# Layer norm's two averages: products of 128 contraction rows, or of 64 on the two halves of the array

## The chip, the cores and the metric

The kernel runs on one core of a Trainium2 chip. A core has TensorE (PE; its weight loads are shown as PEld), VectorE (DVE), ScalarE (ACT), GpSimd (POOL) and SyncE (SP), which run their own instruction streams in order and wait for one another by semaphores. The metric is device time in microseconds, the median of several runs.

## The reference

Input x is 32 images of 128 channels, 32 x 32 points, in fp32. There are two layers, each added to its input:

```python
def _layernorm(x, gamma, beta, eps=1e-05):
    mu = jnp.mean(x, axis=-1, keepdims=True)
    var = jnp.var(x, axis=-1, keepdims=True)
    return (x - mu) * jax.lax.rsqrt(var + eps) * gamma + beta
...
# layer 0, on the group norm of x: u is (32, 128, 1024)
h = jnp.einsum('bdl,de->ble', u, W_enc) + b_enc        # 1024 features
y = gelu(causal convolution of h over the points, 64 taps per feature, + D * h)
g = y @ W_glu + b_glu
g = g[..., :D_MODEL] * jax.nn.sigmoid(g[..., D_MODEL:])
h = _layernorm(h + g, ln_gamma, ln_beta)
out = h @ W_dec + b_dec                                # back to 128 channels
...
# layer 1, on the group norm of the result: a deformable convolution with 64 taps,
# its offsets from a 3 x 3 depthwise convolution, then batch norm and gelu
```

The change concerns `_layernorm` in layer 0: for each of an image's 1024 points, the mean and the mean square over 1024 features.

## The kernel before, in words

A first stage (`ssm_convolution`, up to about 1500 us) makes the convolved features y and puts them into DRAM. Then `main_block` runs two generators side by side: `first_part(b + 2)`, the rest of layer 0 for one image, and `second_part(b)`, the deformable convolution of the image two before it.

`first_part` takes an image in two halves of 512 points (`hf`). A half has eight groups m of 128 features. For each m, TensorE makes the gate (`gpg`, L757, eight matmuls), a decode matmul of the group before (`gpo`, L685), the value (`gpv`, L780, eight matmuls) and the encoding h again (`gph`, L796). ScalarE takes the sigmoid of the gate (L764). VectorE makes gate times value in L788 (`gs`, from `gpv`) and adds h in L809. The result r, 128 features x 512 points, is summed over m on GpSimd: `sums[0]` adds r (L687, in `decode`), and `sums[1]` adds r squared (L818, from ScalarE's square of L817). After eight groups `sums[0]` and `sums[1]` hold, on 128 partitions, partial sums that must still be added over the partitions. `close` does that with two matmuls whose weights `davg` are all 1/1024, so that each of 128 output rows holds the mean: `gpm` (L707) for the mean and `gpq` (L710) for the mean square. ScalarE copies the mean to SBUF (L708) and squares it (L711). The rest of the norm follows in later steps: L714, L717, a root, reciprocals, L726, L729.

A half's `close` is not run at its end but in the next half's group m = 0, after the value's matmuls and L788, and before `gph`. Tile names there: `pglu` has three PSUM banks that gate, value, the two averages and h take in turn. After a close, `gph` and the gate of m = 1 (`gpg`) therefore take the banks that L788 and L708 have read. Temporaries (`temp`) come from five buffers.

`second_part` goes through 68 pieces per image. A piece's weights `ds` (hat functions that ScalarE wrote to DRAM in L953 to L955 and SyncE loads back in L1029) are multiplied by `dhy` on VectorE (L1048). Three matmuls (`dps`, L1091, 208 to 480 columns) go into the four banks of `psam`, VectorE multiplies each by tap weights on the way out (L1094), and GpSimd adds halves (L1111) and then into the image's accumulator (L1116). At the end of an image GpSimd scales the accumulator (L1122) and VectorE adds the input (L1127).

The order of all instructions is that of the program text, under `manual_schedule`. How the two generators interleave is decided by `run_along`: each yields a cost, and the one that has done the smaller share of its total goes on. `MM` is the cost of one 512-column matmul, and

```python
FIRST = 2 * (KD * (2 * KD + 2) + 2) * MM
```

is the total of `first_part`. `tick` runs the steps that `later` has put off by a number of yields.

Of the kernel before, what the change touches and what calls it, by code (L numbers as in the profile page):

```python
# [7 lines left out]
F32 = mybir.dt.float32  # L8
# [6 lines left out]
P = 128  # L15
# [3 lines left out]
KD = D // P  # L19
# [526 lines left out]
def main_block(nc, tc, const, ins, x, u_d, y_d, x1_d, out, offmax):  # L546
# [16 lines left out]
    T = 512  # L563
# [4 lines left out]
    with ctx:  # L568

        def pool(name, bufs, space=None):  # L570
            kw = {} if space is None else {"space": space}
            return ctx.enter_context(tc.tile_pool(name=name, bufs=bufs, **kw))
# [8 lines left out]
        pglu = pool("mb_pg", 3, PSUM)  # L581
# [42 lines left out]
        for k in range(KD):  # L624
            nc.tensor.matmul(
                fold[:, 0:1], w_dec[:, k, :], beta[:, k : k + 1],
                start=(k == 0), stop=(k == KD - 1),
# [32 lines left out]
        MM = 863.0  # L660
# [3 lines left out]
        def load(n, chunks):  # L664

            if n >= len(tiles):
                return
            b, hf = tiles[n]
            cols = slice(hf * T, hf * T + T)
            if n not in loaded:  # L670
                u = two.tile([P, T], F32, tag="gu", name=f"gu_{b}_{hf}")
                nc.sync.dma_start(u, u_d[b, :, cols])
                loaded[n] = u, []
            src = y_d[:, b].rearrange("d j l -> d (j l)")[:, cols]
            for k in chunks:
                y = ypool.tile([P, T], F32, tag="gy", name=f"gy_{b}_{hf}_{k}")
                nc.sync.dma_start(y, src[k * P : (k + 1) * P])
                loaded[n][1].append(y)

        def temp(name):  # L680
            return tpool.tile([P, T], F32, tag="gt", name=name)

        def decode(job):
            m, r, sums, dec = job
            nc.tensor.matmul(dec, w_dec[:, m, :], r, start=(m == 0), stop=(m == KD - 1))  # L685
            if m > 0:
                nc.gpsimd.tensor_add(sums[0], sums[0], r)  # L687
# [7 lines left out]
        def tick():  # L695
            for e in list(soon):
                e[0] -= 1
                if e[0] <= 0:
                    soon.remove(e)
                    e[1]()  # L700

        def close(b, hf, sums, dec, xt):

            tag = f"{b}_{hf}"
            m1, d, rs = (temp(f"g{n}_{tag}") for n in ("m1", "d", "rs"))
            ps = pglu.tile([P, T], F32, tag="g", name=f"gpm_{tag}")
            nc.tensor.matmul(ps, const["davg"], sums[0], start=True, stop=True)  # L707
            nc.scalar.copy(m1, ps)  # L708
            ps = pglu.tile([P, T], F32, tag="g", name=f"gpq_{tag}")
            nc.tensor.matmul(ps, const["davg"], sums[1], start=True, stop=True)  # L710
            nc.scalar.activation(rs, m1, AF.Square)  # L711

            def variance():
                nc.vector.scalar_tensor_tensor(  # L714
                    d, m1, neg_g, dec, op0=ALU.mult, op1=ALU.add
                )
                nc.vector.tensor_sub(rs, ps, rs)  # L717

            def deviation():
                nc.scalar.activation(rs, rs, AF.Sqrt, bias=const["eps"])  # L720

            def invert(lo):
                return lambda: nc.vector.reciprocal(rs[:, lo : lo + P], rs[:, lo : lo + P])

            def scale():
                nc.vector.tensor_mul(d, d, rs)  # L726

            def add():
                nc.vector.scalar_tensor_tensor(xt, d, shift, xt, op0=ALU.add, op1=ALU.add)  # L729

            def store():
                nc.scalar.dma_start(x1_d[b, :, hf * T : hf * T + T], xt)
                stored.add((b, hf))

            later(2, variance)
            later(4, deviation)
            for n in range(4):
                later(7 + n, invert(n * P))
            later(11, scale)
            later(12, add)  # L740
            later(15, store)

        stored = set()
        pending = {}

        def first_part(b, last=False):
            for hf in range(2):
                n = tiles.index((b, hf))
                if n == 0:
                    load(0, range(KD))  # L750
                u, ys = loaded.pop(n)
                sums = dec = xt = None
                for m in range(KD):
                    tag = f"{b}_{hf}_{m}"
                    gate = pglu.tile([P, T], F32, tag="g", name=f"gpg_{tag}")
                    for k in range(KD):
                        nc.tensor.matmul(  # L757
                            gate, w_glu[:, k, D + m * P : D + m * P + P], ys[k],
                            start=(k == 0), stop=(k == KD - 1),
                        )  # L760
                        yield MM
                        tick()
                    sig = temp(f"gs_{tag}")
                    nc.scalar.activation(  # L764
                        sig, gate, AF.Sigmoid, bias=b_glu[:, KD + m : KD + m + 1]
                    )
                    if m == 1:
                        load(n + 1, range(YB - KD))
                        dec = pdec.tile([P, T], F32, tag="dec", name=f"gpo_{b}_{hf}")
                        pending["decode"] = (0, r0, sums, dec)  # L770
                    if m == 4:
                        xt = one.tile([P, T], F32, tag="gx", name=f"gx_{b}_{hf}")
                        nc.sync.dma_start(xt, x[b, :, hf * T : hf * T + T])
                    if "decode" in pending:
                        decode(pending.pop("decode"))
                        yield MM
                        tick()
                    val = pglu.tile([P, T], F32, tag="g", name=f"gpv_{tag}")
                    for k in range(KD):
                        nc.tensor.matmul(  # L780
                            val, w_glu[:, k, m * P : m * P + P], ys[k],
                            start=(k == 0), stop=(k == KD - 1),
                        )
                        if m == KD - 1 and k < 2 * KD - YB:
                            load(n + 1, [YB - KD + k])
                        yield MM
                        tick()
                    nc.vector.scalar_tensor_tensor(  # L788
                        sig, val, b_glu[:, m : m + 1], sig, op0=ALU.add, op1=ALU.mult
                    )  # L790
                    if "close" in pending:
                        close(*pending.pop("close"))
                        yield 2 * MM
                        tick()
                    h = pglu.tile([P, T], F32, tag="g", name=f"gph_{tag}")
                    nc.tensor.matmul(  # L796
                        h, w_enc[:, m * P : (m + 1) * P], u, start=True, stop=True
                    )
                    yield MM
                    tick()  # L800
                    if m == 0:
                        sums = [
                            one.tile([P, T], F32, tag=f"gs{i}", name=f"gs{i}_{b}_{hf}")
                            for i in range(2)
                        ]
                        r = sums[0]
                    else:
                        r = two.tile([P, T], F32, tag="gr", name=f"gr_{tag}")
                    nc.vector.scalar_tensor_tensor(  # L809
                        r, h, b_enc[:, m : m + 1], sig, op0=ALU.add, op1=ALU.add  # L810
                    )
                    if m == 0:
                        nc.scalar.activation(sums[1], r, AF.Square)
                        r0 = r
                    else:
                        sq = temp(f"gq_{tag}")
                        nc.scalar.activation(sq, r, AF.Square)  # L817
                        nc.gpsimd.tensor_add(sums[1], sums[1], sq)  # L818
                        pending["decode"] = (m, r, sums, dec)
                pending["close"] = (b, hf, sums, dec, xt)  # L820
            if last:
                decode(pending.pop("decode"))
                close(*pending.pop("close"))
                while soon:
                    yield MM
                    tick()

        FIRST = 2 * (KD * (2 * KD + 2) + 2) * MM


        images = {}
# [322 lines left out]

        ctx.enter_context(tc.manual_schedule())
        run_along((first_part(0), FIRST))
        run_along((first_part(1), FIRST), (opening(), 90.0))
        for b in range(B):
            steps = prepare(b + 1) if b + 1 < B else []
            if b + 2 < B:  # L1160
                run_along(
                    (first_part(b + 2, last=(b + 2 == B - 1)), FIRST),
                    (second_part(b, steps), SECOND),
# [154 lines left out]
```

## Time and profile before

| | |
|---|---|
| time, median of 3 runs (lowest to highest) | 13582.52 us (13579.27 to 13584.45) |
| the profiled execution: span from first to last instruction | 13587.2 us |
| the profiled execution's own time beside the span | not listed apart; the span is 4.7 us above the median |
| TensorE busy | 13106.8 us, 96% of the span |
| VectorE busy | 8781.8 us, 65% |
| ScalarE busy | 3291.8 us, 24% |
| GpSimd busy | 9080.3 us, 67% |
| mean granted TensorE clock | 0.988 of full speed |
| mean busy share of the DMA engines, 2500 to 13000 us | 0.87 |

How to read the views. In a timeline a row has the start (us from the span's start), the length, the engine, the line, the operation, out<-in, the shape of the tile and a count of merged instructions; in brackets stands the engine's idle time ahead of the row and what ended it. An fp32 matmul appears as two instructions (x2), one for each pass, and a pass's end is modelled, so the pitch from one row's start to the next is a better length for TensorE than the row's own. In the view of waits a row has who waited for whom, the total in us, how many times, and the longest one. In a view of one line the three numbers are the shortest, the median and the longest instruction in ns.

### The profile page before, as it was taken

The page shows a single profiled execution, that of the slowest core. Times are in us where ns is not written, and L with a number is a line of the kernel's source. Part 1 is how long each engine was busy: PE and PEld are TensorE (multiplying, and loading weights), DVE is VectorE, ACT ScalarE, POOL GpSimd, SP SyncE. Part 2 cuts the span into 40 slices and gives each one's busy share as a digit, 9 for nine tenths or more (in the row PEclk, how much of TensorE's full clock was granted, in tenths as well). Part 3 has the DMA queues.
Part 4 walks back from the last instruction along what each step waited for, and adds up shares of the span by engine and source line. Part 5 has one row for each costly group of instructions (what it writes and reads, how often), then busy time and mean ns, then how long its engine had stood idle before and what let it go on. Part 6 is the DMA issues. An engine that isn't in the chain of part 4 may idle for free.

```text
span 13587.2 us, 133930 instructions
## 1 busy us (share of the span) xinstructions
PE 13106.8 (96%) x40482; PEld 7248.5 (53%) x40482; DVE 8781.8 (65%) x12685; ACT 3291.8 (24%) x4767; POOL 9080.3 (67%) x8868
## 2 busy tenths in 40 slices
PE   7999899999999999999999999999999999999975
PEld 7888545555555555555555555555555555555533
DVE  7787226666666666666666666666666666666677
ACT  4333222222211122222222211112222222221145
POOL 2444227777777777777777777777777777777778
PEclk9999999999999999999999999999999999999988
DMA  7888428888888888888889888888888888988876
GB/s 244 275 277 273 132 90 231 234 239 236 231 227 231 233 235 238 238 236 232 230 234 239 235 229 229 231 232 237 238 237 236 232 230 235 240 235 231 230 198 175
DMA packets 1715626, 3105.77 MB, mean 229 GB/s; under 512 B 308306, under 2 KB 1018322, under 8 KB 1713874
## 3 DMA queue, kind: packets, MB, share of 16 engines
q1 hardware_dynamic: 1502290, 2641.91, 73.2%
q10 hardware_dynamic: 163456, 320.92, 6.6%
q0 software_dynamic: 49152, 134.28, 2.9%
q8 instruction: 329, 5.39, 0.2%
q14 instruction: 399, 3.27, 0.1%
HBM read 2630.36 MB, written 466.06 MB: 228 GB/s over the span
## 4 chain that ended last, share of the span: by engine, by line
PE 81%; DMA 9%; DVE 4%; ACT 2%; POOL 2%; issue 1%; SPq 1%; ACTq 0%; DVEq 0%; POOLq 0%
PE gpv L780 24%; PE gpg L757 23%; PE dps L1091 23%; DMA ds<-dhat 4%; PE gph L796 3%; PE gpo L685 3%; PE psy L299 3%; PE psz L223 2%; DMA y_d<-yo 2%; DMA dhat<-dh 2%; DVE z L227 1%; DVE ds L1048 1%; DMA dhy<-dhat 1%; POOL y_d L332 1%; ACT ds L1040 0%
## 5 line engine op out<-in xcount | busy, mean ns | idle before, releaser
L1094 DVE TENSOR_TENSOR dp<-dps,k_weight_slots 128x256 f32<-128x256 f32 (+17 forms) x6528 | 3087.1, 483 | 3109.5 <-PE dps L1091 2914.8
L1091 PE MATMUL dps<-ds,dxw 128*128 128x256 f32 (+18 forms) x13056 | 4701.1, 447 | 223.5 <-DVE ds L1048 177.5
L1116 POOL TENSOR_TENSOR dacc<-dacc,dp 128x256 f32<-128x256 f32 (+3 forms) x4736 | 4417.4, 933 | 396.5 <-DVE dp L1111 26.6
L1091 PEld LDWEIGHTS dps<-ds,dxw 128*128 128x128 f32 x13056 | 2472.7, 192 | 3203.6 <-issue 2537.5
L757 PE MATMUL gpg<-gy,g_w_glu 128*128 128x512 f32 x8192 | 3986.4, 593 | 23.5 <-DMA gy<-y_d 15.7
L780 PE MATMUL gpv<-gy,g_w_glu 128*128 128x512 f32 x8192 | 3975.7, 592 | 0.0
L1111 POOL TENSOR_TENSOR dp<-dp 128x448 f32<-128x448 f32 (+2 forms) x2142 | 2675.1, 1249 | 1882.1 <-DVE dp L1094 1879.4
L1048 DVE TENSOR_TENSOR ds<-ds,dhy 128x1024 f32<-128x1024 f32 (+3 forms) x2176 | 3148.6, 1447 | 762.4 <-DMA ds<-dhat 647.9
L757 PEld LDWEIGHTS gpg<-gy,g_w_glu 128*128 128x128 f32 x8192 | 1546.9, 190 | 1235.8 <-issue 964.9
L780 PEld LDWEIGHTS gpv<-gy,g_w_glu 128*128 128x128 f32 x8192 | 1551.7, 190 | 1155.3 <-issue 913.8
L818 POOL TENSOR_TENSOR gs<-gs,gq 128x512 f32<-128x512 f32 x448 | 628.5, 1403 | 1341.3 <-ACT gq L817 1341.3
L817 ACT ACTIVATE gq<-gr 128x512 f32<-128x512 f32 x448 | 282.3, 630 | 4673.6 <-DVE gr L809 4611.2
L332 POOL DMA_DIRECT2D y_d<-yo x1024 | 590.1, 583 | 869.7 <-ACT yo L320 699.2
L764 ACT ACTIVATE gs<-gpg,k_b_glu 128x512 f32<-128x512 f32 x512 | 351.8, 687 | 2488.0 <-PE gpg L757 2377.6
L953 ACT ACTIVATE dh<-dr,k_minus 128x624 f32<-128x624 f32 x768 | 621.7, 809 | 642.5 <-DMA dhat<-dh 563.1
L299 PE MATMUL psy<-toe,z 128*128 128x192 f32 x4096 | 704.7, 333 | 45.2 <-ACT yo L320 43.8
L299 PEld LDWEIGHTS psy<-toe,z 128*128 128x128 f32 x4096 | 667.5, 192 | 81.6 <-ACT yo L320 74.5
L311 DVE TENSOR_TENSOR psy<-psy,t 32x256 f32<-32x256 f32 (+1 forms) x1280 | 553.7, 433 | 204.7 <-ACT t L307 162.6
L788 DVE SCALAR_TENSOR_TENSOR gs<-gpv,k_b_glu,gs 128x512 f32<-128x512 f32 x512 | 379.7, 742 | 437.3 <-PE gpv L780 437.2
L687 POOL TENSOR_TENSOR gs<-gs,gr 128x512 f32<-128x512 f32 x448 | 634.7, 1417 | 0.0
L954 ACT ACTIVATE dh<-dh,one 128x624 f32<-128x624 f32 x768 | 626.3, 815 | 25.0
L223 PE MATMUL psz<-w_enc,u 128*128 128x128 f32 x4096 | 568.6, 293 | 44.9 <-DVE z L227 32.3
(162 smaller groups left out, 6052.4 us busy)
## 6 DMA issues: line engine op xcount, KB each, us to landing
dhy<-dhat SPq DMA_DIRECT2D x1536, 512.0 KB
ds<-dhat SPq DMA_DIRECT2D x1440, 512.0 KB
dhat<-dh ACTq DMA_DIRECT2D x768, 312.0 KB
y_d<-yo POOLq DMA_DIRECT2D x1024, 128.0 KB, 5.4
gy<-y_d SPq DMA_DIRECT2D x512, 256.0 KB
u<-u_d SPq DMA_DIRECT2D x224, 512.0 KB
toe<-kp_d SPq DMA_DIRECT2D x128, 768.0 KB
dxw<-dvt_d SPq DMA_DIRECT2D x1248, 64.0 KB
```

The lines of the kernel that those rows point to most:

```text
L223: nc.tensor.matmul(ps[:, j, :], u[:, lo : lo + P], w_enc[:, k * P : (k + 1) * P], start=True, stop=True,)
L299: nc.tensor.matmul(ps[:, c // 2, c % 2, :], rows[i][:, g * CG + c0 + c, :], toe[:, c0 + c, :], start=True, stop=True,)
L332: nc.gpsimd.dma_start(y_d[d0 : d0 + CG, :, i * NB + ORDER[j], :].rearrange("d b l -> b d l"), yo[i][j * B : (j + 1) * B],)
L687: nc.gpsimd.tensor_add(sums[0], sums[0], r)
L757: nc.tensor.matmul(gate, w_glu[:, k, D + m * P : D + m * P + P], ys[k], start=(k == 0), stop=(k == KD - 1),)
L780: nc.tensor.matmul(val, w_glu[:, k, m * P : m * P + P], ys[k], start=(k == 0), stop=(k == KD - 1),)
L818: nc.gpsimd.tensor_add(sums[1], sums[1], sq)
L1048: nc.vector.tensor_mul(s[:, :m], s[:, :m], hy[:, :m])
L1091: nc.tensor.matmul(ps, xw[:, j, :], s[:, :m, :, y0 : y0 + ny], start=True, stop=True)
L1094: nc.vector.tensor_mul(prod[:, :m, :, y0 : y0 + ny], ps, w[:, :, :, None].to_broadcast([P, m, KY2, ny]),)
L1111: adder.tensor_add(prod[:, :m, 0], prod[:, :m, 0], prod[:, :m, 1])
L1116: nc.gpsimd.tensor_add(to, to, prod[:, slot : slot + nj, 0])
```

## The change

Before the averages, a new step `halve` folds the running sums onto half of the partitions: ScalarE copies the upper 64 partitions of `sums[0]` to the lower 64 of a temporary, and the lower 64 of `sums[1]` to its upper 64. VectorE adds the temporary onto the lower half of `sums[0]` and onto the upper half of `sums[1]`. The mean is then a matmul over partitions 0 to 63 and the mean square one over partitions 64 to 127. `halve` is called in group m = 0 of the next half, after the fifth of the value's eight matmuls. Both products are recorded ahead of the copy of the mean, `close` yields one `MM` in place of two, and the total `FIRST` goes down with it.

```diff
+        HP = P // 2
+
+        def halve(b, hf, sums, dec, xt):
+
+            other = temp(f"gf_{b}_{hf}")
+            nc.scalar.copy(other[:HP], sums[0][HP:])
+            nc.scalar.copy(other[HP:], sums[1][:HP])
+            nc.vector.tensor_add(sums[0][:HP], sums[0][:HP], other[:HP])
+            nc.vector.tensor_add(sums[1][HP:], sums[1][HP:], other[HP:])
+
         def close(b, hf, sums, dec, xt):
...
-            ps = pglu.tile([P, T], F32, tag="g", name=f"gpm_{tag}")
-            nc.tensor.matmul(ps, const["davg"], sums[0], start=True, stop=True)
-            nc.scalar.copy(m1, ps)
+            pm = pglu.tile([P, T], F32, tag="g", name=f"gpm_{tag}")
             ps = pglu.tile([P, T], F32, tag="g", name=f"gpq_{tag}")
-            nc.tensor.matmul(ps, const["davg"], sums[1], start=True, stop=True)
+            nc.tensor.matmul(pm, const["davg"][:HP], sums[0][:HP], start=True, stop=True)
+            nc.tensor.matmul(ps, const["davg"][HP:], sums[1][HP:], start=True, stop=True)
+            nc.scalar.copy(m1, pm)
             nc.scalar.activation(rs, m1, AF.Square)
...
+                        if m == 0 and k == 4 and "close" in pending:
+                            halve(*pending["close"])
                         yield MM
                         tick()
...
                         close(*pending.pop("close"))
-                        yield 2 * MM
+                        yield MM
                         tick()
...
                 decode(pending.pop("decode"))
+                halve(*pending["close"])
                 close(*pending.pop("close"))
...
-        FIRST = 2 * (KD * (2 * KD + 2) + 2) * MM
+        FIRST = 2 * (KD * (2 * KD + 2) + 1) * MM
```

## The prediction

> **What bounds the kernel now.** I read the page first: span, busy shares, the chain that ended last.
>
> ```profile
> span 13587.2 us, 133930 instructions
> ...
> PE 81%; DMA 9%; DVE 4%; ACT 2%; POOL 2%; issue 1%; SPq 1%; ACTq 0%; DVEq 0%; POOLq 0%
> ```
>
> TensorE holds the end, so any pass taken off it looks like time won. But the two products sit in a place of their own: one "close" per half image, 64 in all. So I asked next what TensorE waits for near them, in the view of waits (total us, times, longest).
>
> ```profile
> PE gph L796 <- DVE gs L788: 30.6, 29, 2.4
> ...
> PE gpg L757 <- DVE gs L788: 7.5, 10, 0.9
> ```
>
> L796 is the matmul right behind the two products, L757 the one behind that. Both wait for VectorE's L788 (gate times value). To see which close waits how, I read the timeline at every close. Apart from the first three and the last there are two kinds, 30 of each.
>
> Kind A closes the first half of an image. TensorE and VectorE at 6246 us:
>
> ```profile
> 6246.27 1.02 PE L707 MATMUL gpm<-gs,davg 128*128 128x512 f32 x2
> 6247.12 1.02 PE L710 MATMUL gpq<-gs,davg 128*128 128x512 f32 x2
> 6247.98 0.66 PE L1091 MATMUL dps<-ds,dxw 128*128 128x288 f32 x2
> 6249.95 1.13 PE L796 MATMUL gph<-gu,k_W_enc 128*128 128x512 f32 x2 [1.31 <-DVE gs L788]
> ```
>
> ```profile
> 6247.18 1.23 DVE L1048 TENSOR_TENSOR ds<-ds,dhy 128x1024 f32<-128x1024 f32 x1 [1.66 <-DMA ds<-dhat]
> 6248.32 0.91 DVE L1094 TENSOR_TENSOR dp<-dps,k_weight_slots 128x256 f32<-128x256 f32 x2
> 6249.16 0.74 DVE L788 SCALAR_TENSOR_TENSOR gs<-gpv,k_b_glu,gs 128x512 f32<-128x512 f32 x1
> ```
>
> The products take 0.85 us each. TensorE is through with them and the 288-column matmul, stands still 1.31 us, and goes on 0.05 us after L788 ends (6249.90). L788 in turn hangs on a DMA that VectorE awaited at L1048.
>
> Kind B closes the second half. VectorE, GpSimd and TensorE at 6431 us:
>
> ```profile
> 6426.95 1.13 DVE L1048 TENSOR_TENSOR ds<-ds,dhy 128x832 f32<-128x832 f32 x1 [0.34 <-DMA ds<-dhat]
> 6428.00 0.38 DVE L1094 TENSOR_TENSOR dp<-dps,k_weight_slots 128x224 f32<-128x224 f32 x1
> 6428.30 1.85 DVE L1127 TENSOR_TENSOR do<-do,dxr 128x1024 f32<-128x1024 f32 x1
> 6430.07 0.58 DVE L1094 TENSOR_TENSOR dp<-dps,k_weight_slots 128x420 f32<-128x420 f32 x1
> 6431.95 0.56 DVE L1094 TENSOR_TENSOR dp<-dps,k_weight_slots 128x390 f32<-128x390 f32 x1 [1.30 <-POOL dacc L1116]
> 6432.44 1.46 DVE L1048 TENSOR_TENSOR ds<-ds,dhy 128x832 f32<-128x832 f32 x1
> 6433.82 0.74 DVE L788 SCALAR_TENSOR_TENSOR gs<-gpv,k_b_glu,gs 128x512 f32<-128x512 f32 x1
> ```
>
> ```profile
> 6427.16 1.91 POOL L1111 TENSOR_TENSOR dp<-dp 128x448 f32<-128x448 f32 x1
> 6429.15 2.78 POOL L1116 TENSOR_TENSOR dacc<-dacc,dp 128x64 f32<-128x64 f32 x4
> ```
>
> ```profile
> 6433.64 1.02 PE L796 MATMUL gph<-gu,k_W_enc 128*128 128x512 f32 x2
> 6434.61 1.13 PE L757 MATMUL gpg<-gy,g_w_glu 128*128 128x512 f32 x2
> ```
>
> L796 would free TensorE at 6434.50; L757 starts at 6434.61, 0.05 us after L788 ends (6434.56). So L788 is late here too, by 0.11 us in this close and by up to 0.94 us in others. The chain behind it is GpSimd (4.72 us for L1111 and L1116), then the evict of 390 columns, L1048, L788. Both kinds go on when L788 ends, not when the products end.
>
> **What the change removes.** Two products of 0.85 us, four passes of 0.43 us one after another (1.71 us). No row shows two products at once. Bounds: all side by side, 0.86 us; as now, 1.71 us. I need not choose, because neither end reaches the clock: in A and B TensorE waits for L788 either way. In A the wait only grows. In B it opens in front of L757. Value on the path: 0. In the first three closes (no second stream beside them) another cover holds: L796 writes the bank that L708 frees, L708 ends 1.65 us after gpm starts, L796 starts at 1.72. At most 0.05 us each is to be had.
>
> The Trainium skill, "TensorEngine Tiling (Array Packing)", Key Properties, says that tiles on different row groups run independently, but that changing the tiling mode drains the array, which speaks against a change that switches twice per close. By the first, the removed part would be worth up to 0.43 to 0.85 us per close if it were on the path; by the second, something goes back. No row here shows either.
>
> **What it moves.** The built programs differ in order: one yield less puts the second stream (dps) one slot later against the first. In A the order becomes gpm, gpq, gph, dps. The 288-column matmul, 0.48 us at the pitch of 0.85 us per 512 columns, now does its work in the wait; after the change it comes behind it: +0.48 us per A. Cover: some 14 us later TensorE stands again for an evict (L1094) that is late through a DMA, 0.5 us or more in 15 of the 29 A closes that I read, 1.02 us in this one. Where it stands, the 0.48 is swallowed. Half of them: 0.24 x 30 = 7 us. SyncE's order changes in 60 or so pairs of loads by one place against gy, gu and gx loads; all are issued ahead, so 0.
>
> **What it adds.** Per close, two ScalarE copies and two VectorE adds, all on 64 partitions x 512.
>
> Copies: nearest row L1040, a copy on 32 partitions, 0.62 us at its shortest. ScalarE sat idle 8 to 9 us before L708 in B; in A the copies stand behind a hat's two activations that end 4 to 8 us before gpm, and ahead of the one that waits for its DMA. They wait for GpSimd's last L687, which ends about 8 us ahead of gpm in A, 3 to 4 in B. VectorE reaches the adds 2 to 3 us ahead of gpm in B, so it waits 0 to 0.3 us for the first copy. Cost 0.
>
> Adds: nearest row L726, two SBUF inputs, 128x512: 691 ns shortest, 1049 longest. Alone two cost 1.4 us, beside a busy GpSimd 2.1.
>
> In A they stand before the idle that ended with the DMA: 1.66 us here, 1.1 to 3.2 elsewhere. They lie in it with at most 0.1 us over on average: 30 x 0.1 = 3 us.
>
> In B they go between L1048 (ends 6428.08) and the evict of 224 columns, with the 1.30 us idle as cover. That is gone (2.0 against 1.30), and the cover is itself GpSimd's lateness, which grows: L1111 of 448 took 1.13 us at 6422.85 beside evicts alone, and 1.91 beside L1048 and L1127. L1111 with its four L1116 took 3.08 us there and 4.72 here, with 2.7 us of VectorE's two-input work beside it: 0.6 us lost for each. Two adds more, 2 us, make GpSimd about 1.1 us later, so the 390-column evict, L1048, L788 and L757 too. Low end: GpSimd loses nothing, 2.0 - 1.30 with adds at 0.7 leaves 0.1 us. High end: adds 2.1 on top of a late sum, 1.5 us. I take 1.0, nearest to the row that shows both engines busy: 30 x 1.0 = 30 us. TensorE has no stall behind it in B that would give it back.
>
> Queued behind the adds on VectorE are the evicts that free the four psam banks; the order leaves three matmuls of slack, so no stall there. The last close (tail) gets the folding in series, about 2 us once, off the chain.
>
> **Sum.** 30 + 7 + 3 = 40 us. On the profiled execution, 13587.2 + 40 = 13627. That span is 4.7 us above the median of the three runs (13582.5), and nothing outside the span changes: 13622 us.
>
> **Rivals.** (1) Hidden: GpSimd does not mind and the idles cover the adds. B 0.1, A 0 to 0.24: 3 to 10 us more, 13586 to 13593. For it: 1.30 us of idle against 1.4 of work. Against: GpSimd's rows of 1.13 and 1.91.
> (2) Faster: the saved pass reaches the end. 64 x 0.43 = 27 us, with both 64 x 0.85 = 55: 13528 to 13555. It decides if L788 ends before the shortened products do, which in none of the 60 closes it does now. It would take a shift of the interleave that clears A's wait.
> (3) Worse: in B the first copy waits on GpSimd's late sum, VectorE stands, and A's 0.48 is nowhere swallowed: B 1.5, A 1.0: 75 us, 13657.
> (4) The change does not do what it says: both products run one after another as now. Then the time is that of my forecast all the same, since the saving is hidden; only the rows would tell.
>
> **How the numbers follow.** About 0.2%, 27 us, is what a measurement of this kernel can tell from no change. Forecast (20 to 60 us) 0.58, hidden 0.27, faster 0.07, worse 0.08. Of the forecast about a tenth lies below 27 us: slower 0.60, same 0.33, faster 0.07. The range reaches from the hidden case's low end to just past the worse case's: 13582 to 13660.
>
> **What would show it.** Right: L788 still the releaser in front of L796 in A, and now of L757 in B, with that second total well above 7.5 us; gpg after gph later in B by about 1 us; adds of 0.7 to 1.05 us; the second product starting 0.43 us or less after the first, or at 0.85, with the same time. GpSimd's L1111 and L1116 in B longer than 4.72 us together. Wrong: L757 and L796 starting without an idle ahead, or the stall in B unchanged at about 0.1 us.

## The result, and the profile after

The changed kernel takes 13624.7 us (median of six runs, 13610.73 to 13640.13) against 13582.52 us before (13579.27 to 13586.29): 42 us slower, ratio 1.0032 with a 95% interval of 1.0021 to 1.0044. That is 0.3%, small but clear of the interval. The forecast was 13622. That it came out within 3 us is partly luck: its terms for the closes of kind A were wrong, and what they left out largely cancelled; the experiments take this apart.

The profiled execution of after is the slowest of its six, so its span is 51 us above that of before. Its span and busy times:

```profile
span 13638.4 us, 134143 instructions
...
PE 13118.4 (96%) x40482; PEld 7231.1 (53%) x40482; DVE 8953.8 (66%) x12813; ACT 3367.4 (25%) x4895; POOL 9179.3 (67%) x8868
```

VectorE does 172 us more work than before (adds, and slower neighbours) and GpSimd 99 us more with the same instructions. TensorE's products became shorter and its busy time still went up by 12 us.

In after, line numbers have moved: the copies are L707 and L708, the adds L709 and L710, the products L718 and L719, and old L757, L788, L796, L1048, L1094, L1111 and L1116 are now L767, L800, L808, L1061, L1107, L1124 and L1129. The view of waits of after (who waits for whom: total us, times, longest):

```profile
PE gph L808 <- DVE gs L800: 62.7, 30, 2.9
PE gpg L767 <- DVE gs L800: 32.1, 28, 1.8
...
PE dps L1104 <- DVE dp L1107: 4.4, 8, 1.5
```

The first row was 30.6 us, the second 7.5. Gate times value (L800) is still the releaser in A, and now also in front of `gpg` 28 times, with the close shown next as the pattern, as the prediction asked. The third row, TensorE's second stall some 14 us behind an A close, was 31.1 us (51 times) before.

A close of kind B in the timeline of after (start, length, engine, line; in brackets the idle time ahead and what ended it):

```profile
6440.64 1.91 POOL L1124 TENSOR_TENSOR dp<-dp 128x448 f32<-128x448 f32 x1
...
6441.49 1.61 DVE L709 TENSOR_TENSOR gs<-gs,gf 64x512 f32<-64x512 f32 x1
...
6442.63 3.66 POOL L1129 TENSOR_TENSOR dacc<-dacc,dp 128x64 f32<-128x64 f32 x4
6443.13 0.70 DVE L710 TENSOR_TENSOR gs<-gs,gf 64x512 f32<-64x512 f32 x1
...
6444.72 0.69 PE L718 MATMUL gpm<-gs,davg 64*128 64x512 f32 x1
6444.73 0.69 PE L719 MATMUL gpq<-gs,davg 64*128 64x512 f32 x1
6445.25 0.59 PE L718 MATMUL gpm<-gs,davg 64*128 64x512 f32 x1
6445.26 0.59 PE L719 MATMUL gpq<-gs,davg 64*128 64x512 f32 x1
...
6446.33 0.56 DVE L1107 TENSOR_TENSOR dp<-dps,k_weight_slots 128x390 f32<-128x390 f32 x1 [0.44 <-POOL dacc L1129]
...
6448.19 0.74 DVE L800 SCALAR_TENSOR_TENSOR gs<-gpv,k_b_glu,gs 128x512 f32<-128x512 f32 x1
...
6448.98 1.12 PE L767 MATMUL gpg<-gy,g_w_glu 128*128 128x512 f32 x2 [0.88 <-DVE gs L800]
```

The two products lie on each other: the second starts 0.01 us after the first, and the next pair of passes 0.53 us later, so all four passes take 1.06 us in place of 1.71. Nothing comes of it. On VectorE one of the adds takes 1.61 us; GpSimd's L1124 and L1129, beside them, take 5.65 us from first start to last end, where L1111 and L1116 took 4.77; the 390-column evict waits for them, L800 ends at 6448.93, and `gpg` starts 0.05 us later after an idle of 0.88.

A close of kind A (TensorE alone), and the granted clock there (per stretch: length, busy times, PEclk, DMA share, GB/s):

```profile
6259.16 1.12 PE L718 MATMUL gpm<-gs,davg 64*128 64x512 f32 x2
6260.12 1.12 PE L719 MATMUL gpq<-gs,davg 64*128 64x512 f32 x2
6263.29 2.07 PE L808 MATMUL gph<-gu,k_W_enc 128*128 128x512 f32 x2 [2.05 <-DVE gs L800]
6265.16 1.16 PE L1104 MATMUL dps<-ds,dxw 128*128 128x288 f32 x2
```

The stretches:

```profile
6256.00:6262.00 6.00, 5.24 (x14) 1.98 (x12) 5.94 (x8) 2.85 (x4) 3.97 (x3) 1.00 0.64 228
6262.00:6263.30 1.30, 0.01 (x1) 0.01 (x1) 1.24 (x3) 0.00 (x0) 0.97 (x2) 0.81 0.80 180
6263.30:6265.10 1.80, 1.80 (x2) 0.83 (x3) 0.00 (x0) 0.00 (x0) 1.64 (x3) 0.50 1.01 273
```

Here the second add was still running when the first product was ready, so the products ran one after the other (15 of the 64 closes do so; in 36 the second starts within 0.1 us). What no step of the prediction had is the last row. TensorE stands for 2.05 us, its clock falls to 0.50, and `gph` takes 1.87 us (6263.29 to 6265.16) where it otherwise takes 0.86. The clock records of after hold 22 such falls between 1500 and 13000 us, 88.7 us in all, each 3.41 us or twice that. Before has none there. At half speed that is 44 us of TensorE's work, and at most as much time: a part of a fall can lie in the stand itself, and a later stall can swallow the delay.

### The profile page after: what moved, and what is told of

It is laid out like the page before. It is cut to its first block, busy times and chain, and to the rows that moved or that the text cites. A ratio compares the mean times of both kernels' runs of the same rounds, so it can differ in the third digit from the quotient of the medians.

```text
span 13638.4 us, 134143 instructions
## 1 busy us (share of the span) xinstructions
PE 13118.4 (96%) x40482; PEld 7231.1 (53%) x40482; DVE 8953.8 (66%) x12813; ACT 3367.4 (25%) x4895; POOL 9179.3 (67%) x8868
## 5 line engine op out<-in xcount | busy, mean ns | idle before, releaser
L1107 DVE TENSOR_TENSOR dp<-dps,k_weight_slots 128x256 f32<-128x256 f32 (+17 forms) x6528 | 3101.4, 483 | 3337.3 <-PE dps L1104 3027.0
L1129 POOL TENSOR_TENSOR dacc<-dacc,dp 128x256 f32<-128x256 f32 (+3 forms) x4736 | 4444.3, 938 | 394.4 <-DVE dp L1124 24.5
L767 PE MATMUL gpg<-gy,g_w_glu 128*128 128x512 f32 x8192 | 4004.6, 594 | 49.4 <-DVE gs L800 32.1
L1124 POOL TENSOR_TENSOR dp<-dp 128x448 f32<-128x448 f32 (+2 forms) x2142 | 2698.7, 1260 | 1689.0 <-DVE dp L1107 1681.0
L1061 DVE TENSOR_TENSOR ds<-ds,dhy 128x1024 f32<-128x1024 f32 (+3 forms) x2176 | 3155.2, 1450 | 493.0 <-DMA ds<-dhat 392.4
L767 PEld LDWEIGHTS gpg<-gy,g_w_glu 128*128 128x128 f32 x8192 | 1552.0, 190 | 1252.3 <-issue 962.7
L830 POOL TENSOR_TENSOR gs<-gs,gq 128x512 f32<-128x512 f32 x448 | 684.1, 1527 | 1495.2 <-ACT gq L829 1495.0
L800 DVE SCALAR_TENSOR_TENSOR gs<-gpv,k_b_glu,gs 128x512 f32<-128x512 f32 x512 | 379.5, 741 | 384.8 <-PE gpv L790 384.7
```

What stands on the lines that cost most here:

```text
L767: nc.tensor.matmul(gate, w_glu[:, k, D + m * P : D + m * P + P], ys[k], start=(k == 0), stop=(k == KD - 1),)
L1061: nc.vector.tensor_mul(s[:, :m], s[:, :m], hy[:, :m])
L1107: nc.vector.tensor_mul(prod[:, :m, :, y0 : y0 + ny], ps, w[:, :, :, None].to_broadcast([P, m, KY2, ny]),)
L1124: adder.tensor_add(prod[:, :m, 0], prod[:, :m, 0], prod[:, :m, 1])
L1129: nc.gpsimd.tensor_add(to, to, prod[:, slot : slot + nj, 0])
```

## The experiments

Every experiment keeps the rest of the kernel. To compare them closer than the times allow I measured, in each profile, the mean distance from one close to the next, 29 distances of each sort: from an A close to the B close after it (this holds what A costs, and what is won back behind it), and from a B close to the next A. The anchor in each is the fifth value matmul, recorded ahead of everything that the change adds. The 29 distances of one kernel scatter (standard deviation 0.5 to 1.4 us), so a mean is uncertain by 0.1 to 0.26 us: the differences in the column of B are clear, small ones in the column of A are not. "Falls" are those of the clock between 1500 and 13000 us.

| kernel | time, us | against before, same chip [95%] | A to B, us | B to A, us | falls |
|---|---|---|---|---|---|
| before | 13582.52 | | 184.05 | 184.05 | 0 |
| after | 13624.7 | 1.0032 [1.0021, 1.0044] | 185.06 | 184.95 | 22 |
| change_again | 13632.82 | 1.0032 [1.0020, 1.0044] | 184.79 | 184.94 | 20 |
| order_only | 13578.3 | 1.0000 [0.9991, 1.0009] | 183.98 | 183.89 | 4 |
| no_fold_keep | 13579.36 | 0.9997 [0.9988, 1.0006] | 184.40 | 184.05 | 8 |
| no_fold | 13583.95 | 1.0003 [0.9994, 1.0012] | 184.13 | 183.96 | 11 |
| fold_beside | 13590.65 | 1.0003 [0.9994, 1.0012] | 183.80 | 184.75 | 5 |
| keep_order | 13595.84 | 1.0010 [1.0001, 1.0019] | 183.75 | 184.93 | 7 |
| adds_only | 13616.04 | 1.0019 [1.0010, 1.0028] | 184.31 | 184.94 | 2 |
| copies_only | 13556.08 | 0.9979 [0.9970, 0.9988] | 183.29 | 183.98 | 3 |
| filler | 13607.44 | 1.0018 [1.0008, 1.0027] | 183.68 | 184.71 | 2 |
| psum_fold | 13586.11 | 1.0003 [0.9993, 1.0012] | 184.45 | 184.04 | 16 |
| psum_fold_keep | 13551.79 | 0.9978 [0.9968, 0.9987] | 182.96 | 183.95 | 2 |
| psum_beside | 13549.71 | 0.9973 [0.9963, 0.9983] | 183.00 | 184.02 | 1 |

**The order alone (order_only).** The products of before, with the change's yields:

```diff
-                        yield 2 * MM
+                        yield MM
...
-        FIRST = 2 * (KD * (2 * KD + 2) + 2) * MM
+        FIRST = 2 * (KD * (2 * KD + 2) + 1) * MM
```

> The kernel before with close yielding 1 MM and FIRST smaller by as much: only the interleave of the change. Theory 1: A pays 0.24 to 0.5 us x 30 = 7 to 15 us, with few low-clock stretches since the products still take 1.71 us. Theory 2: 25 to 40 us.

Measured: 13578.3 us, no difference, so both theories missed. The 288-column matmul moved behind `gph` costs nothing by itself: TensorE reaches the next stall later and stands there for less. That stall, first in before and then in order_only:

```profile
PE dps L1091 <- DVE dp L1094: 31.1, 51, 2.7
```

```profile
PE dps L1091 <- DVE dp L1094: 17.8, 32, 1.2
```

**The products alone, in the old order (no_fold_keep) and in the new (no_fold).** The change without its fold, in no_fold_keep also with the old yields:

```diff
-                        if m == 0 and k == 4 and "close" in pending:
-                            halve(*pending["close"])
...
-                halve(*pending["close"])
                 close(*pending.pop("close"))
```

> Only the two products of 64 rows; copies and adds are left out (so the means are of half the features), interleave as before. Theory 1 (the saved passes lie in front of a wait for L788 and are worth nothing): within 8 us of before. Rival (the saved passes reach the end and the fold costs the more): 64 x 0.66 = 42 us less than before, 0.66 us being what the first three closes show. The products should still start together.

> The products of 64 rows and the interleave of the change; copies and adds left out (means of half the features). Theory 1: B at before's time; A waits longer than before (0.48 us moved, 0.66 us saved, so about 2 us) but not later L788: 5 to 15 low-clock stretches, 5 to 20 us above before. Rival (without the adds nothing is lost): within 5 us of before.

Measured: 13579.36 and 13583.95 us, neither to be told from before. Four passes in 1.06 us in place of 1.71, in all 64 closes, are worth nothing on the clock. The rival that the saved passes reach the end, 27 to 55 us, is refuted. In no_fold the clock falls 11 times although the kernel only does less: the falls that theory 1 forecast (5 to 15), with the time of its rival (within 5 us of before). So 41 us of low clock cost no time that can be seen there.

**The fold alone (fold_beside) and the change in the old order (keep_order).** fold_beside runs copies and adds into a temporary and leaves the products over 128 rows of the sums themselves:

```diff
-            nc.vector.tensor_add(sums[0][:HP], sums[0][:HP], other[:HP])
-            nc.vector.tensor_add(sums[1][HP:], sums[1][HP:], other[HP:])
+            nc.vector.tensor_add(other[:HP], sums[0][:HP], other[:HP])
+            nc.vector.tensor_add(other[HP:], sums[1][HP:], other[HP:])
```

> The kernel before, with the two copies and two adds of the folding made beside it into the temporary, products over 128 rows as before, interleave as before. Theory 1: B pays 0.85 us x 30 = 26 us for the adds, A little: 20 to 32 us above before. Rival (the fold is hidden and it is the products' wait for it that costs): 0 to 8 us.

keep_order is the change with the old yields:

```diff
-                        yield MM
+                        yield 2 * MM
...
-        FIRST = 2 * (KD * (2 * KD + 2) + 1) * MM
+        FIRST = 2 * (KD * (2 * KD + 2) + 2) * MM
```

> The whole change, but close yields 2 MM and FIRST has its old total, so that the two streams interleave as before. Theory 1 (kind B pays for the adds, which slow GpSimd while GpSimd holds up L788; kind A pays for the moved 288-column matmul and for the low clock behind its longer wait): B's 0.85 us x 30 = 26 us stay, A's part goes: 20 to 32 us above before. Theory 2 (the shifted interleave and the low clock make nearly all of it): 0 to 10 us above before. Low-clock stretches in the main block: theory 1 and 2 both under 8, against 22 with the change.

Measured: 13590.65 and 13595.84 us. In B they cost nearly what the change costs (184.75 and 184.93 against 184.95), so B's price is the fold's. The times fit neither theory well: fold_beside is 9 us above its own before, under theory 1's 20 to 32, and keep_order 14, between the ranges of its two theories (with 7 falls, as both had it). In A both are shorter than before, by 0.25 and 0.30 us, hardly more than the scatter. The prediction's sum had no gain there; if something in the fold wins time in A, its halves must show it.

**The fold's two halves (copies_only, adds_only).** copies_only has the two ScalarE copies and no adds (first diff, against the change); adds_only has two adds of the same shape straight from the sums and no copies (second); both keep the products and the order of before.

```diff
             nc.scalar.copy(other[:HP], sums[0][HP:])
             nc.scalar.copy(other[HP:], sums[1][:HP])
-            nc.vector.tensor_add(sums[0][:HP], sums[0][:HP], other[:HP])
-            nc.vector.tensor_add(sums[1][HP:], sums[1][HP:], other[HP:])
```

```diff
-            nc.scalar.copy(other[:HP], sums[0][HP:])
-            nc.scalar.copy(other[HP:], sums[1][:HP])
-            nc.vector.tensor_add(sums[0][:HP], sums[0][:HP], other[:HP])
-            nc.vector.tensor_add(sums[1][HP:], sums[1][HP:], other[HP:])
+            nc.vector.tensor_add(other[:HP], sums[0][:HP], sums[1][:HP])
+            nc.vector.tensor_add(other[HP:], sums[0][HP:], sums[1][HP:])
```

> The kernel before with only the two ScalarE copies beside it. Theory C (the copies, by holding back the next hat's store, bring the loads forward in kind A): the weights' multiply behind A's close starts 1.5 to 2.5 us earlier after the fifth value matmul than the 14.2 us of before, 0 to 20 us faster. Theory V (it is the adds): as before, 14.2 us, time within 6 us.

> The kernel before with only two VectorE adds over 64 partitions beside it, of the two sums, both in SBUF. Theory V: the weights' multiply behind A's close starts 1.5 us earlier than before's 14.2 us, and B pays 0.75 us x 30 = 22 us. Theory C: 14.2 us as before, and B pays the same: 15 to 30 us above before.

Measured: the copies make the kernel 31 us faster than before, the adds make it 29 us slower. The adds' share is 0.89 us per B close and 0.26 per A close, 30 x 1.15 = 34 us by these distances. In the waits of adds_only TensorE's stall in B is there at full size without any copy and without any new product:

```profile
PE gpg L765 <- DVE gs L798: 31.1, 28, 1.8
```

The copies' share is -0.76 us per A close and nothing in B. It shows at TensorE's second stall behind A, here in copies_only (31.1 us, 51 times before, as shown above):

```profile
PE dps L1102 <- DVE dp L1105: 8.6, 23, 1.1
```

That stall hangs on the weights `ds` of a piece, and their multiply behind an A close (the first that starts more than 8 us after the start of the fifth value matmul) starts 14.24 us after it with the copies, 15.24 before and 15.31 in adds_only. The 14.2 us that the expectations give for before is too small, since in some closes it took the multiply of an earlier piece; theory C was right in kind, with 1.0 us for its 1.5 to 2.5, and with 31 us in time where it had at most 20. One link ahead of the multiply is visible. SyncE's queue holds the load of a piece's image window (`dxw`, L1062) until ScalarE's hats have landed in DRAM, and other loads stand behind it. The waits of SyncE's queue, first in before:

```profile
SPq L1062 <- DMA dhat<-dh: 274.3, 60, 9.0
```

and in copies_only, where the line is L1073:

```profile
SPq L1073 <- DMA dhat<-dh: 209.0, 56, 7.2
```

So this load and what is behind it go out earlier. It holds in every kernel: behind A the load goes out 4.00 to 4.22 us after the start of the fifth value matmul in the nine kernels with the copies, and 4.94 to 5.13 in the five without, adds_only (4.97, wait 268.6 us) among them. The hat's store ahead of it is issued at the same place (0.29 us ahead of that matmul in copies_only, 0.45 before), so it is not held back, as theory C had it; it lands sooner. Why two copies on ScalarE, 1.2 us of work, make it land sooner the runs do not show.

**The fold with one operand in PSUM (psum_fold).** One word of the change decides where the copies land: a bank of `psam` in place of SBUF.

```diff
-            other = temp(f"gf_{b}_{hf}")
+            other = psam.tile([P, T], F32, tag="sam", name=f"gf_{b}_{hf}")
```

> The whole change, with the temporary of the folding in a PSUM bank of dps in place of SBUF, so that each add reads one operand from SBUF and one from PSUM. Theory 1 (two SBUF operands beside GpSimd slow both, and in B GpSimd holds L788): in B the two adds take 1.4 us in place of 2.2, GpSimd's L1116 falls from 3.7 to about 2.8 us, L788 is less late by 0.5 to 0.85 us, 15 to 26 us faster than the change. Rival (it is the adds' place in VectorE's order): B unchanged, 42 us above before.

Measured: 13586.11 us, 4 above its own before where the change is 42 above its own: more than the 15 to 26 us that theory 1 had, and its rival is refuted. B is back at 184.04. VectorE's groups of the adds, first in after (count | busy us, mean ns of one | idle before):

```profile
L710 DVE TENSOR_TENSOR gs<-gs,gf 64x512 f32<-64x512 f32 x64 | 73.9, 1155 | 2.0
...
L709 DVE TENSOR_TENSOR gs<-gs,gf 64x512 f32<-64x512 f32 x64 | 68.4, 1068 | 19.0 <-ACT gf L707 19.0
```

In psum_fold:

```profile
L710 DVE TENSOR_TENSOR gs<-gs,gf 64x512 f32<-64x512 f32 x64 | 44.3, 692 | 2.0
...
L709 DVE TENSOR_TENSOR gs<-gs,gf 64x512 f32<-64x512 f32 x64 | 43.1, 674 | 32.9 <-ACT gf L708 32.9
```

With two operands in SBUF an add takes 0.67 to 1.66 us by what GpSimd does beside it; with one in PSUM the longest of all 128 is 0.69. The price in B was this contention, not the adds' own length. The Trainium skill says so ("GPSIMD Engine Reference", section 1, Specifications, the table's row on SBUF interfaces: shared with VectorE, contended by VectorE instructions with two SBUF inputs); these rows agree, and give it a size. In A psum_fold still pays (184.45), with 16 falls of the clock.

**A product that nobody needs (filler).** The change with the second product run a third time, 0.86 us of TensorE's time in the place where it would stand:

```diff
             nc.tensor.matmul(ps, const["davg"][HP:], sums[1][HP:], start=True, stop=True)
+            nc.tensor.matmul(ps, const["davg"][HP:], sums[1][HP:], start=True, stop=True)
```

> The whole change, with the product for the mean square made a second time into the same bank: 0.86 us more of TensorE work per close, nothing else. Theory 1 (in kind A TensorE now stands so long that its clock is halved for 3.4 us, and that is what A costs; B costs 26 us by the adds): the wait in A falls by 0.86 us, the low-clock stretches fall from 22 to under 8, and the kernel gets faster by 20 to 35 us, to about 10 to 20 us above before. Rival (the moved 288-column matmul itself is what A costs): low-clock stretches or not, 42 us above before or more, up to 64 x 0.86 = 55 us more.

Measured: 13607.44 us. Each against its own before, filler is 25 us above, the change 42 and its repeat 46: 17 to 21 us less with more work per close. Theory 1 is right in kind and its 20 to 35 us a little too high; its rival, more time, is refuted. An A close of filler in TensorE's timeline:

```profile
6254.52 1.02 PE L720 MATMUL gpq<-gs,davg 64*128 64x512 f32 x2
...
6256.66 1.12 PE L809 MATMUL gph<-gu,k_W_enc 128*128 128x512 f32 x2 [1.13 <-DVE gs L801]
...
6258.12 1.02 PE L768 MATMUL gpg<-gy,g_w_glu 128*128 128x512 f32 x2
```

TensorE stands 1.13 us in place of 2.05, `gph` runs at full speed, and the falls go from 22 to 2. A to B goes from 185.06 to 183.68 us. A product more cannot bring anything behind it forward, so the gain is put down to the clock. B to A fell too, by 0.24 us; that is about the scatter and is not explained. The profiled execution of filler is the fastest of its eleven, so the medians, which differ by less, are the safer size: 17 to 21 us.

**The repeat (change_again)**, to see whether the falls belong to one execution:

> The change once more, beside the runs that follow: 13610 to 13640 us, 30 to 55 above before, if the low-clock stretches of the other kernels' traces are what sets them apart, with 15 or more such stretches; lower, with fewer, would say that the place of the clock's window decides from run to run.

Measured: 13632.82 us, 20 falls, 78.5 us of low clock, the same two distances within 0.3 us. They belong to the program.

**Versions that win (psum_fold_keep, psum_beside).** psum_fold_keep is psum_fold with the old yields: the change's products, no contention, and the stall kept short. psum_beside keeps the products over 128 rows and the order of before, and puts the folded sums into a temporary that nobody reads:

```diff
-            other = temp(f"gf_{b}_{hf}")
+            other = psam.tile([P, T], F32, tag="sam", name=f"gf_{b}_{hf}")
+            done = temp(f"ge_{b}_{hf}")
...
-            nc.vector.tensor_add(sums[0][:HP], sums[0][:HP], other[:HP])
-            nc.vector.tensor_add(sums[1][HP:], sums[1][HP:], other[HP:])
+            nc.vector.tensor_add(done[:HP], sums[0][:HP], other[:HP])
+            nc.vector.tensor_add(done[HP:], sums[1][HP:], other[HP:])
```

> The same with the PSUM temporary, and the interleave as before. Theory 1: B's loss and A's are both gone: 10 us below to 5 us above before. Rival (adds' place): 14 us above before, as with the old interleave alone.

> The kernel before with copies and adds made beside it, the copies into a PSUM bank of dps, products over 128 rows as before, interleave as before. Theory P (the 31 us that the PSUM version with the old interleave gains come from the shortened products): within 8 us of before. Theory S (they come from a side effect of the folding, by which SyncE's loads in kind A land some 2 us earlier and TensorE's second stall there goes): 15 to 30 us less than before, without any shorter product.

Measured: 13551.79 and 13549.71 us, 31 and 37 us faster than before, clear of their intervals, and both more than the theories had (at most 10 and 30 us). psum_fold_keep is a version of the change that beats both kernels. What wins is not its products, since psum_beside does without them and copies_only, which has neither the new products nor the adds, is nearly as fast at 13556.08.

## Why the prediction was right, and where it was not

**What TensorE waits for: right.** L800 releases `gph` in A and `gpg` in B, 0.05 us before each, and the saved passes only lengthen the wait. no_fold_keep measures the saving at 2 us, not to be told from the 0 of the prediction. Rival 4 is refuted (the products do run side by side) and made no difference, as it said. What changing the tiling twice per close costs is not to be seen as a time of its own. One small point failed: in the first three closes, `gph` did not wait for the copy of the mean. It now starts 1.06 us after `gpm` in place of 1.72, so 0.66 us is had there and not "at most 0.05", three times only.

**B: right, mechanism and size.** 1.0 us per close was forecast, 0.90 measured (adds_only 0.89). The steps hold one by one at the close shown: the adds take 2.3 us (one of them 1.61, over the 1.05 that was forecast as the most); GpSimd's pair takes 0.88 us longer (1.1 forecast); the evict, L1061, L800 and `gpg` follow. psum_fold shows that without the contention B costs 0. Three figures of the working are slips that change nothing: the low end for B is 1.4 - 1.30, not 2.0 - 1.30; GpSimd's pair took 4.77 us by the rows, not 4.72; and the hidden case ends at 13586, so the range begins lower than its low end, at the time of before.

**A: wrong in three terms.** 0.34 us per close was forecast, 1.01 measured (0.74 in the repeat).
- The moved matmul was put at 0.24 us; order_only gives -0.07. The stall behind it swallows all of it, not half, as far as the scatter lets one see.
- The copies were put at 0 ("ScalarE sat idle") and are worth -0.76. I looked for who waits for the copies and found nobody; I did not ask what they move on the queues. ScalarE's next hat does not come later by them: it starts 4.01 us after the start of the fifth value matmul, against 4.95 before.
- The stall in A "only grows" was priced at nothing. It grew from 1.02 to 2.09 us on average, and the clock fell: 21 of the 22 falls belong to an A close. Their 88.7 us cost at most half of that, 44 us, or 1.48 per A close.

The adds were put at 0.1 us and come to 0.26, a difference within the scatter. These terms together come near the case: -0.07 - 0.76 + 0.26 + 1.48 = 0.91 against 1.01 measured; for the repeat, with 78.5 us of low clock, 0.74 against 0.74; for filler, with its 2 falls, -0.46 against -0.37. The agreement is better than the sum deserves. order_only, copies_only and adds_only have falls of their own, worth 0.23, 0.17 and 0.11 us by the same rule, which the sum counts twice; without them it gives 0.40 for the change. And it misses no_fold and psum_fold_keep by about half a microsecond. So it shows the direction of each term, and not that the sizes add up. In the times it is as loose: copies and adds together should give -2 us, and fold_beside measures 9 above its own before.

So the total of 40 us stood on 30 that were right, 10 that were put at the wrong places, and two terms that were not in the sum and largely offset each other: a gain of 23 (profile) to 31 us (time) from the copies, a loss of 17 to 21 (filler's time) to at most 44 us (the falls) from the clock. That these came out at nearly the forecast is luck. Rival 3 (75 us) is far off; rival 1 (hidden) falls with B. The rival that was missing is a faster TensorE that waits so long that it is slowed afterwards.

**The clock.** The Trainium skill, "TensorE: Matmul & The Clock Gate", Part 1, has an activity window of about 3.4 us that runs free, and half clock after a window or more of idleness. The falls here agree with the window: they last 3.41 us or 6.83, and their starts lie on a grid of it (5894.17 and 6262.81 are 108 windows of 3.413 apart). They differ in what it takes: the stands at the falls in A last 2.0 to 2.9 us, and the fall begins 1.2 to 3.7 us after TensorE has come to rest. Shorter stands were enough too: 1.2 us at both falls of filler, 1.36 us at five of the seven in keep_order. Nor does every stand lead to one: stands of 2 us or more number 27 in after, with 22 falls, and 2 in before, with none. So no length that decides can be read from these runs. That the place of the stand on the grid decides is argued, not shown.

## What to carry to other kernels

When an engine waits at the end of a piece of work, making that work shorter buys nothing, and on TensorE a stand that grows, here from 1 us to 2, can cost more than the work saved: look at the granted clock right behind every wait that a change lengthens. An operation of VectorE with both inputs in SBUF is paid twice where GpSimd is busy and late (here up to 1.66 us for an add of 0.67, and 0.88 us more for GpSimd's pair); with one input in PSUM neither engine was slowed (GpSimd 9078.5 us busy in psum_fold_keep, 9080.3 before). And an "idle" engine that issues or feeds transfers is not free to fill in either direction: add the work to it alone and measure, before it is entered in the sum as 0.

## What was not expected of the hardware

- TensorE's clock fell after stands of about 2 us, and in other kernels of 1.2 to 1.4 us, on a fixed grid of 3.41 us. Taking away 20 of the 22 falls with a useless product won 17 to 21 us of the 42; in no_fold 11 falls cost nothing that can be seen.
- Two fp32 products of 64 rows run side by side in 1.06 us where two of 128 rows take 1.71: a gain of 1.6 times, not 2, a pair of passes taking 0.53 us against 0.43 for one pass. If their inputs come 1 us apart, they run one after the other.
- Two copies of 0.62 us on ScalarE made the kernel 31 us faster. The load of the image window goes out 0.94 us earlier and SyncE's wait ahead of it falls from 274.3 to 209.0 us; what shortens it stays open. It was not tried to move those hats or loads by hand.
